# A new opening, a relieved VectorE at the convolution's end, and a later place for two sign conversions in a four-block transformer kernel

## The chip, the cores and the metric

The kernel runs on one core of a Trainium2 chip. The metric is device time in microseconds, lower is better. Before the change it takes 740.42 us (median of three runs, 739.88 to 740.97).

A core has five engines with a queue of instructions each, taken in order: TensorE (PE, matmuls and transposes), VectorE (DVE), ScalarE (ACT), GpSimd (POOL), and SyncE (SP), which here only issues DMAs. PEld is TensorE's loading of weights. Engines wait for each other by semaphores. Matmul results go to PSUM; everything else lies in SBUF or in device memory.

## The reference

The input `x` is 8 x 256 x 512, that is 2048 rows of 512. Four blocks follow each other, each added to x through the tanh of a gate:

```python
x = x + jnp.tanh(g_xattn[0]) * conv(ctx, ctx, layernorm(x), ssm_kernel, D)   # 32 heads of 8 channels
x = x + jnp.tanh(g_ffn[0]) * ffn0(layernorm(x), w1, w2, w3)                  # ternary weights, int8 rows
x = x + jnp.tanh(g_xattn[1]) * attention(layernorm(x), ctx, mask)            # 256 keys per batch
x = x + jnp.tanh(g_ffn[1]) * ffn1(layernorm(x), w1, w2, w3)                  # sign weights, int8 groups of 64
```

`conv` forms the products k_i * v_j of the 8 channels of a head, convolves each causally with the head's kernel of length 512, adds D times the product, multiplies by q (here the normalised x) and sums over i. `ffn0` is `(silu(a(x) W1) * (a(x) W2)) W3`; `a` rounds a row to int8 by its largest magnitude, and weights are rounded to -1, 0, 1 by their mean magnitude.

## The kernel before, in words

x lies in SBUF as 16 row tiles `xs[:, t, :]` of 128 rows. The even tiles hold the first half of each batch's sequence and feed heads 0 to 15, the odd ones feed heads 16 to 31.

**Opening (L606 to L713).** Eight even tiles are needed before the first head can be multiplied by q: each is loaded (`load_x`, in pairs), gets mean and variance on VectorE (`pair_stats`, L116 and L117), a root on ScalarE (`pair_sqrt`), a reciprocal and a bias on VectorE (`pair_inverse`), is normalised (`pair_norm` on ScalarE, or `ln_apply` on VectorE, L174), transposed by TensorE (`pair_turn`, L387) and copied from PSUM into `qT` (`pair_keep`). `load_ch` loads a head's context, `ctx_twice` (ScalarE, L290) and `pair_products` (GpSimd, L303 and L309) make its 36 products `kv`. `toep` is a Toeplitz view of a head's kernel, 128 x 512. Head 0 reads it from the input and gets D on its diagonal by `first_diagonal`; the others read `ssm_skip`, a copy in device memory to which D has been added. The written order of these calls is the order on every engine, since scheduling is manual (L217).

**Convolution (L716 to L748).** One pass per head h, with these calls in order: loads for h+3 and h+4; `q_twice(h+1)` and `ctx_twice(h+3)` on ScalarE, `pair_products(h+3)` on GpSimd; `half_products(h, 1)` on VectorE (three multiplies of y in PSUM by q, L348, L354, L361); the reduction of head h-1 on VectorE (L376), after `add_halves` on GpSimd (L371) had added the two halves of `prod`; heads 12, 14, 19 and 21 (`alone`) have no `add_halves` and one longer reduction on VectorE in their own pass (L378); `half_matmuls(h+1, 1)`, `half_wrap(h+1, 1)` (ScalarE, L336), `half_products(h+1, 0)`, `half_matmuls(h+2, 0)`, `half_wrap(h+2, 0)`. There are three PSUM buffers for y, so a half's matmuls wait for the VectorE products of the half three before. Between these calls stand jobs by head and slot (`job`, `run`): loading, summing and rounding of the ffn0 weights (`abs_w0`, `round_w0` on ScalarE, `clip_w0` on GpSimd), sums of ffn1 weights, odd tiles, adding finished tiles back to x, and towards the end the first rows of ffn0 (`front_norm`, `front_max`, `front_int`, `front_turn`) and statistics of eight tiles (`first_stats`, `ln_moments_of`).

**ffn0 (L923 to L1014).** One step per row tile t, 17 steps. Each has three `up_block` calls (TensorE L792, silu on ScalarE L800, gate on VectorE L801), the rounding of the row before (`row_max` on VectorE, int8 on ScalarE L942, `qh` in bf16 on GpSimd L960, a transposing DMA `hqT` L962), `down0` of the row two before (L809), and the front of the row two after. `ln_finish` makes inverse roots for four tiles by three Newton steps of small GpSimd instructions (L159 to L165). From step 3 on two 512-wide pieces of ffn1 weights are loaded per step (`w1_signs`) and turned into signs on ScalarE a step later (L780). Step 16 (t == NT) only rounds the last row and opens attention.

**Attention and ffn1 (L1118 to L1360)** are touched only by the order in which signs arrive.

Of the kernel before, what the change touches and what calls it, by code (L numbers as in the profile page):

```python
# [42 lines left out]
def flamingo_gated_kernel(  # L43
# [47 lines left out]
    nc.gpsimd.memset(ln_eps, LN_EPS)  # L91
    gates_in = small.tile([P, 4], F32, name="gates_in")
    gates = const.tile([P, 4], F32, name="gates")
# [148 lines left out]
    ssm = big.tile([H, P + L], F32, name="ssm")  # L242
    skip = big.tile([H, 1], F32, name="skip")
    d0 = big.tile([P, 1], F32, name="d0")

# [39 lines left out]
    def first_diagonal():  # L285
        t = toeps[0][:, :P]
        nc.vector.scalar_tensor_tensor(t, anti, d0[:, 0:1], t, op0=ALU.mult, op1=ALU.add)

# [84 lines left out]
    def reduce_terms(h, added):  # L373
# [3 lines left out]
        else:  # L377
            nc.vector.tensor_reduce(  # L378
                o, prod.rearrange("p k a j d -> p (a j) k d"), AX.XY, ALU.add
            )  # L380
# [70 lines left out]
    def clip_w0(i, k):  # L451
# [48 lines left out]
    def front_int(k):  # L500
        i80[k] = pf1.tile([P, L], I8, tag="i8x", name="i8x")
        nc.scalar.activation(i80[k], xn0.pop(k), AF.Copy, scale=am0[k][1])
# [68 lines left out]
    for i, (a, b, c) in enumerate(STEPS0):
        for k in range(NL):
            job(a + k, "load", load_w0, i, k)
            job(b + k, "act", abs_w0, i, k)
            job(c[k], "act", round_w0, i, k)
            job(c[k] if i < 2 else (29, 30, 31, 31)[k], "pool", clip_w0, i, k)
# [17 lines left out]
    for k in range(2):  # L594
# [3 lines left out]
        job(28 + k, "pool", front_turn, k)  # L598
    for k in range(GRP, 2 * GRP):
        job(24 + k, "dve", ln_moments_of, st0, order0, k, "0")  # L600

# [3 lines left out]

    for g, o in ((g_xattn, 0), (g_ffn, 2)):  # L606
        nc.scalar.dma_start(out=gates_in[:, o : o + 2], in_=g.partition_broadcast(P))
    nc.scalar.dma_start(out=d0, in_=ssm_d[0:1].partition_broadcast(P))
    nc.scalar.dma_start(out=ssm, in_=ssm_pad)
    nc.scalar.dma_start(out=skip, in_=ssm_d.rearrange("(h o) -> h o", o=1))  # L610
    pairs = [evens[k : k + 2] for k in range(0, len(evens), 2)]
    load_x(pairs[0])
    load_ch(0)
    first_toep()
    for k in range(1, len(pairs)):
        load_x(pairs[k])
    load_ch(1)
    load_table(AF.Tanh)
    nc.scalar.activation(gates, gates_in, AF.Tanh)
    load_table(AF.Sqrt)  # L620

    ps_ = {}
# [8 lines left out]

    def pair_inverse(k, by_act):

        mv, std = ps_[k]
        rstd = ln_inverse(std, 2, "p")
        nmr = ln_nmr(nc.vector, mv, rstd, by_act, "p")
        both = wl.tile([P, 3 * L], F32, tag="w0st", name="xnp")
        xn = [both[:, :L], both[:, L : 2 * L]]
        for j in range(2):
            if j not in by_act:  # L640
                ln_apply(xn[j], pairs[k][j], mv, rstd, j)
        ps_[k] = (xn, rstd, nmr)

    def pair_norm(k, by_act):
        xn, rstd, nmr = ps_[k]
        for j in by_act:
            ln_apply_act(xn[j], pairs[k][j], rstd, nmr, j)

    def pair_turn(k, js=(0, 1)):
        for j in js:  # L650
            transpose_x(pairs[k][j], ps_[k][0][j])

# [7 lines left out]
    pair_stats(0, 0)  # L660
    pair_stats(0, 1)
    ctx_twice(0)
    pair_products(0)
    pair_sqrt(0)
    pair_stats(1, 0)
    pair_inverse(0, (0, 1))
    pair_norm(0, (0, 1))
    first_diagonal()
    pair_stats(1, 1)
    pair_turn(0)  # L670
    pair_sqrt(1)
    half_matmuls(0, 0)
    nc.vector.tensor_add(ssm[:, P : P + 1], ssm[:, P : P + 1], skip)
    nc.sync.dma_start(out=ssm_skip, in_=ssm)
    load_toep(1)
    load_ch(2)
    load_toep(2)
    load_ch(3)
    pair_stats(2, 0)
    pair_keep(0, 0, nc.scalar)  # L680
    pair_inverse(1, (0,))
    pair_norm(1, (0,))
    pair_keep(0, 1, nc.scalar)
    pair_stats(2, 1)
    pair_turn(1, (1, 0))
    pair_sqrt(2)
    pair_stats(3, 0)
    half_matmuls(0, 1, (0,))
    pair_keep(1, 1, nc.scalar)
    pair_inverse(2, (0,))  # L690
    pair_norm(2, (0,))
    pair_stats(3, 1)
    pair_turn(2, (1, 0))
    pair_sqrt(3)
    pair_keep(1, 0, nc.scalar)
    pair_inverse(3, (0,))
    pair_norm(3, (0,))
    ctx_twice(1)
    pair_products(1)
    pair_keep(2, 1, nc.vector)  # L700
    half_wrap(0, 0)
    pair_turn(3, (1, 0))
# [13 lines left out]
    for h in range(H):  # L716
# [206 lines left out]
    for t in range(NT + 1):  # L923
# [484 lines left out]
```

## Time and profile before

| what | value |
|---|---|
| median of three runs | 740.42 us |
| the profiled execution | 740.89 us |
| its span, first to last instruction | 739.1 us |
| convolution, TensorE busy from 40 to 100 us | 58.85 of 60 us |
| the same from 160 to 220 us | 54.41 of 60 us |
| the same from 300 to 330 us | 26.41 of 30 us |
| the same from 420 to 440 us | 20.00 of 20 us |
| DMA rate from 5 to 10 us | 346 GB/s |

The span is 1.8 us shorter than the execution; what lies around it belongs to the start and end of the program. A row of the timeline gives the start, the duration, the engine and source line, the operation, the tile written and the tiles read with their shapes, and how many were merged. In brackets stands how long the engine had been idle before it and what ended that. "q" behind an engine's name means its sequencer, which issues DMAs. A busy TensorE is not always a fast one: equal matmuls can be compared by their duration.

### The profile page before, as it was taken

Reading aid. Unit: us, or ns where it says so; the run is one execution under the profiler, and the core shown is the slowest. Engines: PE = TensorE matmul, PEld = TensorE weight load, DVE = VectorE, ACT = ScalarE, POOL = GpSimd, SP = SyncE. Lnnn points to the kernel's source line nnn. Section 1 sums busy time; section 2 is a strip of 40 time slices with the busy share of each in tenths; the row PEclk is TensorE's granted clock in tenths of the full one; section 3 lists DMA queues with packets and bytes.
Section 4 is the critical chain, followed back from the end, with each engine's and each line's share of the span. In section 5 each row is a group of like instructions: output and inputs, shape, how many; then the busy total and the mean of one; then the engine's idle time right before and its main releaser. Section 6 shows DMA issues by size and latency. Waiting matters only on the chain.

```text
span 739.1 us, 10041 instructions
## 1 busy us (share of the span) xinstructions
PE 711.0 (96%) x3172; PEld 528.3 (71%) x3172; DVE 605.0 (82%) x1232; ACT 363.7 (49%) x640; POOL 255.8 (35%) x360
## 2 busy tenths in 40 slices
PE   4999999999899999989999999999999999999997
PEld 3777777776454444556677788888888888888885
DVE  4799878898988889667777999888889888777965
ACT  5477877765577777758851223222223322222322
POOL 2898988888885444343310010000200002000000
PEclk9999999999999999999999999999999999999999
DMA  5675676831055557778613455445444545553443
GB/s 193 208 234 173 186 255 197 270 96 43 15 84 137 138 138 157 167 232 254 200 57 55 101 122 125 96 108 118 108 95 97 121 90 118 109 115 82 109 88 85
DMA packets 150444, 99.36 MB, mean 134 GB/s; under 512 B 84280, under 2 KB 128312, under 8 KB 150392
## 3 DMA queue, kind: packets, MB, share of 16 engines
q1 hardware_dynamic: 149608, 98.38, 51.3%
q0 software_dynamic: 256, 0.26, 0.5%
q8 instruction: 25, 0.41, 0.2%
q14 instruction: 27, 0.22, 0.1%
q10 hardware_dynamic: 528, 0.08, 0.1%
HBM read 75.58 MB, written 5.03 MB: 109 GB/s over the span
## 4 chain that ended last, share of the span: by engine, by line
PE 66%; DVE 4%; DMA 3%; issue 1%; POOL 1%; ACT 1%; SPq 0%; DVEq 0%; ACTq 0%; POOLq 0%
PE po L1283 16%; PE pb L1098 15%; PE pa L1098 15%; PE po L809 4%; PE po L907 4%; PE pb L792 4%; PE pa L792 4%; PE ps L878 3%; DMA hqT<-qh 1%; DMA w1st<-in_L_w2t 1%; DMA sT<-d 1%; PE tr L867 1%; DVE hh L801 1%; DVE st L116 0%; DVE qT L376 0%
## 5 line engine op out<-in xcount | busy, mean ns | idle before, releaser
L326 PE MATMUL y<-kv,toep 128*128 128x288 f32 x640 | 162.5, 411 | 4.4 <-DVE prod L361 4.2
L326 PEld LDWEIGHTS y<-kv,toep 128*128 128x128 f32 x640 | 120.3, 192 | 37.7 <-issue 2.0
L1106 ACT ACTIVATE sl<-pa,wmean 128x512 f32<-128x512 f32 x64 | 44.0, 688 | 187.2 <-PE pa L1098 187.2
L1098 PE MATMUL pa<-w,hi 128*128 128x512 f32 x256 | 100.7, 393 | 0.0
L1098 PE MATMUL pb<-w,hi 128*128 128x512 f32 x256 | 99.9, 390 | 0.6 <-DVE hh L1110 0.6
L1283 PE MATMUL po<-w,lo 128*128 128x512 f32 x256 | 100.0, 391 | 0.0
L1283 PE MATMUL po<-w,hi 128*128 128x512 f32 x256 | 99.8, 390 | 0.0
L1098 PE MATMUL pa<-w,lo 128*128 128x512 f32 x256 | 99.7, 390 | 0.0
L1098 PE MATMUL pb<-w,lo 128*128 128x512 f32 x256 | 99.7, 389 | 0.0
L159 POOL TENSOR_TENSOR nwt<-rstd 128x4 f32<-128x4 f32 x33 | 6.5, 198 | 240.5 <-DVE rstd L154 238.8
L303 POOL TENSOR_TENSOR kv<-cx 128x1024 f32<-128x1024 f32 x32 | 60.6, 1893 | 33.9 <-ACT cx L290 33.9
L371 POOL TENSOR_TENSOR prod<-prod 128x1024 f32<-128x1024 f32 x28 | 66.2, 2363 | 2.7 <-DVE prod L361 2.7
L792 PEld LDWEIGHTS <-xqT 128*128 128x128 bf16 x384 | 37.4, 98 | 41.4 <-issue 4.5
L1073 ACT CAST hi<-v 128x512 fp32r<-128x512 f32 x64 | 39.1, 621 | 48.6 <-DVE v L1273 48.6
L1110 DVE SCALAR_TENSOR_TENSOR hh<-pb,wmean,sl 128x512 f32<-128x512 f32 x64 | 47.7, 746 | 14.1 <-PE pb L1098 14.1
L1098 PEld LDWEIGHTS pb<-w,hi 128*128 128x128 f32 x256 | 48.1, 188 | 11.0 <-DVE hh L1110 1.0
L1283 PEld LDWEIGHTS po<-w,lo 128*128 128x128 f32 x256 | 48.1, 188 | 10.8 <-DVE lo L1078 1.0
L1098 PEld LDWEIGHTS pa<-w,hi 128*128 128x128 f32 x256 | 48.1, 188 | 10.3 <-issue 0.5
L1098 PEld LDWEIGHTS pa<-w,lo 128*128 128x128 f32 x256 | 48.1, 188 | 10.3 <-DVE lo L1078 0.2
L1283 PEld LDWEIGHTS po<-w,hi 128*128 128x128 f32 x256 | 48.1, 188 | 9.9
L1098 PEld LDWEIGHTS pb<-w,lo 128*128 128x128 f32 x256 | 48.1, 188 | 9.9
L348 DVE TENSOR_TENSOR prod<-y,qx 128x512 f32<-128x512 f32 x64 | 43.6, 681 | 10.9 <-ACT y L336 7.1
(142 smaller groups left out, 1325.3 us busy)
## 6 DMA issues: line engine op xcount, KB each, us to landing
sT<-d SPq DMA_DIRECT2D x64, 256.0 KB
toep<-ssm_skip SPq DMA_DIRECT2D x31, 256.0 KB
ch<-in_ctx_heads SPq DMA_DIRECT2D x32, 128.0 KB
w1a<-in_L_w1t SPq DMA_DIRECT2D x8, 512.0 KB
w1a<-in_L_w2t SPq DMA_DIRECT2D x8, 512.0 KB
w1st<-in_L_w1t SPq DMA_DIRECT2D x16, 256.0 KB
w1st<-in_L_w2t SPq DMA_DIRECT2D x16, 256.0 KB
cT<-in_ctx_t SPq DMA_DIRECT2D x8, 512.0 KB
```

Of the source, the lines that this page charges most:

```text
L303: nc.gpsimd.tensor_tensor(kv[:, :, 0 : ND * HD].rearrange("p a (i d) -> p a i d", d=ND), cx[:, :, 0:HD].unsqueeze(3).to_broadcast([P, NL * ...
L326: nc.tensor.matmul(y[:, k, :, W0 : W0 + NPAIR], toeps[h][:, d * P : (d + 1) * P], kvs[h][:, mi * B : (mi + 1) * B, :].rearrange("p b n -> ...
L348: nc.vector.tensor_tensor(prod[:, 0, r, :, :], yv[:, :, W0 : W0 + ND * HD].rearrange("p a (i d) -> p a i d", d=ND), view(q, [HX, n], [1, H ...
L371: nc.gpsimd.tensor_tensor(flat[0], flat[0], flat[1], ALU.add)
L792: nc.tensor.matmul(pp[:, :fw], xqT[:, c, :], w0q[i][:, c, f0 : f0 + fw], start=(c == 0), stop=(c == NL - 1),)
L809: nc.tensor.matmul(po, hqT[:, c, :], w0q[2][:, c, :], start=(c == 0), stop=(c == NF0 - 1))
L907: nc.tensor.matmul(po, eT[:, c, :], cN[:, c, :], start=(c == 0), stop=(c == S // P - 1))
L1073: nc.scalar.copy(hi, v)
L1098: nc.tensor.matmul(pp, xT[k][:, c, :], w1q[i][:, c, f0 : f0 + 512], start=(c == 0 and k == 0), stop=(c == NL - 1 and k == 1),)
L1106: nc.scalar.activation(sl, pa, AF.Silu, scale=wmean1[:, 0:1])
L1110: nc.vector.scalar_tensor_tensor(hh, pb, wmean1[:, 1:2], sl, op0=ALU.mult, op1=ALU.mult)
L1283: nc.tensor.matmul(po, hT[b][k][:, c, :], w1q[2][:, b * NL + c, :], start=(b == 0 and c == 0 and k == 0), stop=(b == NB - 1 and c == NL - ...
```

## The change

It has six parts.

- Opening, loads: the two gate broadcasts, the broadcast of D[0] and the column `skip` are replaced by three loads into one row, `singles`; two small matmuls spread it over partitions (`wide`). The x pairs are issued ahead of `toep` of head 0.
- Opening, work: 18 matmuls of `ident` by itself on TensorE (`warm`), with nothing that reads their result. `pair_norm` puts a tile on ScalarE, GpSimd or VectorE; tiles (1,1) and (2,1) go to GpSimd. The tanh of the gates moves into the first head's pass.
- Reductions of the heads in `alone` move one pass later; the last head's reduction moves from VectorE in ffn0's first step to GpSimd in the last pass (`reduce_last`).
- Statistics of four tiles move from VectorE (passes 28 to 31) to ScalarE (passes 24, 25, 28, 29; `moments_by_act`, five instructions a tile).
- The second `i8x` gets a tile of its own; the last `clip_w0` becomes a Sign on ScalarE.
- ffn0: `down0` of row 0 moves behind the third `up_block` of step 2; the pending signs of step 16 are made in attention's first step; `batch_gate` moves from step 15 to step 16.

```diff
+    def moments_by_act(got, order, k, tag, junk):
+        g, j = k // GRP, k % GRP
+        if g not in got:
+            got[g] = small.tile([P, GRP, 2], F32, tag="mv" + tag, name="mv")
+        mean, var = got[g][:, j, 0:1], got[g][:, j, 1:2]
+        v = xs[:, order[k], :]
+        st = small.tile([P, nc.vector.BN_STATS_DIM], F32, tag="st", name="st")
+        nc.scalar.activation(junk, v, AF.Identity, accum_out=st[:, 0:1])
+        nc.scalar.activation(st[:, 1:2], st[:, 0:1], AF.Copy, scale=-1.0 / L)
+        nc.scalar.activation(junk, v, AF.Square, bias=st[:, 1:2], accum_out=st[:, 2:3])
+        nc.scalar.activation(mean, st[:, 0:1], AF.Copy, scale=1.0 / L)
+        nc.scalar.activation(var, st[:, 2:3], AF.Copy, scale=1.0 / L)
...
+    def reduce_last(h):
+        prod, o = prods.pop(h), qT[:, :, h * HD : (h + 1) * HD]
+        half = prod[:, 1, :, :, 0:2]
+        nc.gpsimd.tensor_tensor(half, prod[:, 0, :, :, 0:2], prod[:, 0, :, :, 2:4], ALU.add)
+        nc.gpsimd.tensor_tensor(o, half[..., 0], half[..., 1], ALU.add)
...
+    def clip_by_act(i, k):
+        n, a = FW[i][k], sum(FW[i][:k])
+        q = w0q[i].rearrange("p c f -> p (c f)")
+        nc.scalar.activation(q[:, a : a + n], w0r.pop((i, k))[:, :n], AF.Sign)
...
-        i80[k] = pf1.tile([P, L], I8, tag="i8x", name="i8x")
+        i80[k] = (big if k == 1 else pf1).tile([P, L], I8, tag="i8x", name="i8x")
...
+    job(0, "act", tanh_gates)
+    job(1, "act", load_table, AF.Sqrt)
...
-    for k in range(GRP, 2 * GRP):
-        job(24 + k, "dve", ln_moments_of, st0, order0, k, "0")
+    for k, h in enumerate((24, 25, 28, 29)):
+        job(h, "late", first_by_act, GRP + k)
...
-    for g, o in ((g_xattn, 0), (g_ffn, 2)):
-        nc.scalar.dma_start(out=gates_in[:, o : o + 2], in_=g.partition_broadcast(P))
-    nc.scalar.dma_start(out=d0, in_=ssm_d[0:1].partition_broadcast(P))
     nc.scalar.dma_start(out=ssm, in_=ssm_pad)
-    nc.scalar.dma_start(out=skip, in_=ssm_d.rearrange("(h o) -> h o", o=1))
+    for v, o in ((ssm_d, 4), (g_xattn, 0), (g_ffn, 2)):
+        n = v.shape[0]
+        nc.scalar.dma_start(out=singles[:, o : o + n], in_=v.rearrange("(o n) -> o n", o=1))
     pairs = [evens[k : k + 2] for k in range(0, len(evens), 2)]
     load_x(pairs[0])
     load_ch(0)
-    first_toep()
     for k in range(1, len(pairs)):
         load_x(pairs[k])
+    first_toep()
     load_ch(1)
-    load_table(AF.Tanh)
-    nc.scalar.activation(gates, gates_in, AF.Tanh)
     load_table(AF.Sqrt)
+    pt = ps_tr.tile([P, 512], F32, tag="tr", name="warm")
+    def warm(n):
+        for _ in range(n):
+            nc.tensor.matmul(pt[:, :P], ident, ident, start=True, stop=True)
+    warm(8)
+    wide = ps_tr.tile([P, 512], F32, tag="tr", name="wide")
+    nc.tensor.matmul(wide[:, : 4 + H], ones[0:1, :], singles, start=True, stop=True)
+    nc.tensor.matmul(
+        wide[:H, 64:65], singles[:, 4 : 4 + H], ones[0:1, 0:1], start=True, stop=True
+    )
+    warm(10)
...
     pair_stats(0, 0)
     pair_stats(0, 1)
+    nc.vector.tensor_copy(wide_sb, wide[:, : 4 + H])
+    nc.vector.tensor_add(ssm[:, P : P + 1], ssm[:, P : P + 1], wide[:H, 64:65])
+    nc.sync.dma_start(out=ssm_skip, in_=ssm)
     ctx_twice(0)
     pair_products(0)
...
-        if h > 0 and h - 1 not in alone:
-            reduce_terms(h - 1, True)
-        if h in alone:
-            reduce_terms(h, False)
-        else:
+        if h > 0:
+            reduce_terms(h - 1, h - 1 not in alone)
+        if h not in alone:
             add_halves(h)
...
+        if h == H - 1:
+            reduce_last(h)
         run(h, "pool")
...
             load_table(AF.Exp)
-            for make in signs:
-                make()
-            signs = []
+            gates3 = {0: batch_gate(negs[0])}
...
-        if t >= 2:
+        if t > 2:
             hqT, f3 = hq_.pop(t - 2)
             d_[t - 2] = (down0(hqT), f3)
...
+        if t == 2:
+            hqT, f3 = hq_.pop(0)
+            d_[0] = (down0(hqT), f3)
...
         if t == 0:
-            reduce_terms(H - 1, True)
+            clip_by_act(2, 3)
...
-        for make in signs:
-            make()
-        signs = []
+        if t < NT:
+            for make in signs:
+                make()
+            signs = []
...
-            gates3 = {0: batch_gate(negs[0])}
```

The rest of the opening after `pair_products(0)` is written anew, in this order of TensorE's work: turns of tiles (0,0), (0,1), (1,1), (1,0), the first half of head 0, turn (2,1), a third of its second half, turns (2,0), (3,1), (3,0), and the rest of head 0. Before, it was turns (0,0), (0,1), the first half, turns (1,1), (1,0), part of the second, then the turns of pairs 2 and 3 and the rest.

More of the change, by code (lines that the diff above doesn't have):

```diff
@@ L91, in flamingo_gated_kernel @@
     nc.gpsimd.memset(ln_eps, LN_EPS)
-    gates_in = small.tile([P, 4], F32, name="gates_in")
+    const.tile([P, 24], F32, name="lines")
     gates = const.tile([P, 4], F32, name="gates")
@@ L242, in flamingo_gated_kernel @@
     ssm = big.tile([H, P + L], F32, name="ssm")
-    skip = big.tile([H, 1], F32, name="skip")
-    d0 = big.tile([P, 1], F32, name="d0")
+    singles = big.tile([1, 4 + H], F32, name="singles")
+    wide_sb = big.tile([P, 4 + H], F32, name="wide_sb")
+    d0 = wide_sb[:, 4:5]
     anti = wl.tile([P, 3 * L], F32, tag="w0st", name="anti")[:, :P]
@@ L286, in first_diagonal @@
         t = toeps[0][:, :P]
-        nc.vector.scalar_tensor_tensor(t, anti, d0[:, 0:1], t, op0=ALU.mult, op1=ALU.add)
+        nc.vector.scalar_tensor_tensor(t, anti, d0, t, op0=ALU.mult, op1=ALU.add)
     def twice(out, src):
@@ L566, in flamingo_gated_kernel, with tanh_gates @@
         job(k + 5, "act", keep_x, odds[k])
+    def tanh_gates():
+        load_table(AF.Tanh)
+        nc.scalar.activation(gates, wide_sb[:, 0:4], AF.Tanh)
+    job(0, "act", tanh_gates)
+    job(1, "act", load_table, AF.Sqrt)
     for k in range(len(evens)):
@@ L575, in flamingo_gated_kernel @@
             job(c[k], "act", round_w0, i, k)
-            job(c[k] if i < 2 else (29, 30, 31, 31)[k], "pool", clip_w0, i, k)
+            if (i, k) != (2, 3):
+                job(c[k] if i < 2 else (29, 30, 31)[k], "pool", clip_w0, i, k)
         job(b + NL - 1, "dve", total_w0, i)
@@ L598, in flamingo_gated_kernel, with first_by_act @@
         job(28 + k, "pool", front_turn, k)
-    for k in range(GRP, 2 * GRP):
-        job(24 + k, "dve", ln_moments_of, st0, order0, k, "0")
-    for g, o in ((g_xattn, 0), (g_ffn, 2)):
-        nc.scalar.dma_start(out=gates_in[:, o : o + 2], in_=g.partition_broadcast(P))
-    nc.scalar.dma_start(out=d0, in_=ssm_d[0:1].partition_broadcast(P))
+    def first_by_act(k):
+        junk = p2.tile([P, L], F32, tag="xn", name="junk")
+        moments_by_act(st0, order0, k, "0", junk)
+    for k, h in enumerate((24, 25, 28, 29)):
+        job(h, "late", first_by_act, GRP + k)
     nc.scalar.dma_start(out=ssm, in_=ssm_pad)
-    nc.scalar.dma_start(out=skip, in_=ssm_d.rearrange("(h o) -> h o", o=1))
+    for v, o in ((ssm_d, 4), (g_xattn, 0), (g_ffn, 2)):
+        n = v.shape[0]
+        nc.scalar.dma_start(out=singles[:, o : o + n], in_=v.rearrange("(o n) -> o n", o=1))
     pairs = [evens[k : k + 2] for k in range(0, len(evens), 2)]
@@ L630, in pair_sqrt, with pair_inverse, pair_norm, pair_turn @@
         ps_[k] += (ln_sqrt(ps_[k][0], 2, "p"),)
-    def pair_inverse(k, by_act):
+    def pair_inverse(k):
         mv, std = ps_[k]
         rstd = ln_inverse(std, 2, "p")
-        nmr = ln_nmr(nc.vector, mv, rstd, by_act, "p")
+        nmr = ln_nmr(nc.vector, mv, rstd, range(2), "p")
         both = wl.tile([P, 3 * L], F32, tag="w0st", name="xnp")
[L638 to L644, printed above, removed]
+        ps_[k] = ([both[:, :L], both[:, L : 2 * L]], rstd, nmr)
+    def pair_norm(k, j, eng):
         xn, rstd, nmr = ps_[k]
-        for j in by_act:
+        if eng is nc.scalar:
             ln_apply_act(xn[j], pairs[k][j], rstd, nmr, j)
-    def pair_turn(k, js=(0, 1)):
-        for j in js:
-            transpose_x(pairs[k][j], ps_[k][0][j])
+        else:
+            c = slice(j, j + 1)
+            eng.tensor_scalar(
+                xn[j], xs[:, pairs[k][j], :], rstd[:, c], nmr[:, c], ALU.mult, ALU.add
+            )
+    def pair_turn(k, j):
+        transpose_x(pairs[k][j], ps_[k][0][j])
     def pair_keep(k, j, eng):
@@ L664, in flamingo_gated_kernel @@
     pair_sqrt(0)
+    pair_inverse(0)
+    pair_norm(0, 0, nc.scalar)
+    pair_norm(0, 1, nc.scalar)
     pair_stats(1, 0)
-    pair_inverse(0, (0, 1))
-    pair_norm(0, (0, 1))
+    pair_stats(1, 1)
+    pair_turn(0, 0)
+    pair_turn(0, 1)
+    pair_sqrt(1)
+    pair_stats(2, 0)
+    pair_inverse(1)
+    pair_keep(0, 0, nc.scalar)
+    pair_keep(0, 1, nc.scalar)
+    pair_norm(1, 1, nc.gpsimd)
+    pair_norm(1, 0, nc.scalar)
+    pair_stats(2, 1)
     first_diagonal()
-    pair_stats(1, 1)
-    pair_turn(0)
-    pair_sqrt(1)
+    pair_turn(1, 1)
+    pair_turn(1, 0)
     half_matmuls(0, 0)
-    nc.vector.tensor_add(ssm[:, P : P + 1], ssm[:, P : P + 1], skip)
-    nc.sync.dma_start(out=ssm_skip, in_=ssm)
     load_toep(1)
@@ L678, in flamingo_gated_kernel @@
     load_ch(3)
[L679 to L685, printed above, removed]
     pair_sqrt(2)
     pair_stats(3, 0)
-    half_matmuls(0, 1, (0,))
[L689 to L693, printed above, removed]
-    pair_sqrt(3)
[L695 to L702, printed above, removed]
+    pair_inverse(2)
+    pair_keep(1, 1, nc.scalar)
+    pair_keep(1, 0, nc.scalar)
+    pair_norm(2, 1, nc.gpsimd)
+    ctx_twice(1)
+    pair_norm(2, 0, nc.scalar)
+    pair_products(1)
+    pair_stats(3, 1)
+    pair_turn(2, 1)
+    half_matmuls(0, 1, (0,))
+    pair_turn(2, 0)
+    pair_sqrt(3)
+    pair_inverse(3)
+    pair_norm(3, 1, nc.vector)
+    pair_norm(3, 0, nc.scalar)
+    pair_keep(2, 1, nc.scalar)
+    pair_turn(3, 1)
+    pair_turn(3, 0)
     pair_keep(2, 0, nc.vector)
-    pair_keep(3, 1, nc.scalar)
-    pair_keep(3, 0, nc.vector)
+    pair_keep(3, 1, nc.vector)
+    pair_keep(3, 0, nc.scalar)
     half_matmuls(0, 1, (1,))
     q_twice(0)
+    half_wrap(0, 0)
     half_wrap(0, 1)
```

## The prediction

> **What bounds the kernel now.** I read the page's busy table first, then the waits of TensorE, then the timeline around each place where TensorE stands still.
>
> ```profile
> span 739.1 us, 10041 instructions
> ...
> PE 711.0 (96%) x3172; PEld 528.3 (71%) x3172; DVE 605.0 (82%) x1232; ACT 363.7 (49%) x640; POOL 255.8 (35%) x360
> ```
>
> TensorE is the bound: a change gains only what it takes out of TensorE's standstill, or out of time in which TensorE runs slowly. The timeline shows four places. First the opening:
>
> ```profile
> 0.73 0.46 SPq L260 DMA_DIRECT2D xs<-in_x  x1
> ...
> 4.30 2.26 SPq L260 DMA_DIRECT2D xs<-in_x  x3
> ...
> 5.68 0.69 DVE L116 BATCH_NORM_STATS2 st<-xs 128x6 f32<-128x512 f32 x1 [5.68 <-DMA xs<-in_x]
> ...
> 8.73 0.69 DVE L116 BATCH_NORM_STATS2 st<-xs 128x6 f32<-128x512 f32 x1 [1.35 <-DMA xs<-in_x]
> ...
> 10.93 1.94 PE L387 MATMUL tr<-ident,xnp 128*128 128x128 f32 x8 [10.93 <-ACT xnp L179]
> ...
> 12.66 3.09 PE L326 MATMUL y<-kv,toep 128*128 128x288 f32 x6
> ...
> 17.09 1.62 PE L326 MATMUL y<-kv,toep 128*128 128x288 f32 x6
> ...
> 22.71 0.69 DVE L348 TENSOR_TENSOR prod<-y,qx 128x512 f32<-128x512 f32 x1 [0.74 <-ACT qx L290]
> ```
>
> TensorE does nothing for 10.9 us; then six equal matmuls take 3.09 us and later 1.62 us: it runs at half speed until about 16.9 us, though the clock column reads 1.00. From 21.08 us it is full. The second and third row pairs are issued 3 us after the loads before them: SyncE stood until an earlier load had landed.
>
> Second, the heads in `alone`, where VectorE does two reductions in a row before the product that frees a y buffer (TensorE's waits, us, times, longest; then the timeline):
>
> ```profile
> PE y L326 <- DVE prod L361: 4.2, 6, 1.5
> ```
> ```profile
> 136.24 1.22 DVE L376 TENSOR_REDUCE qT<-prod 128x256 f32<-128x1024 f32 x1 [1.74 <-POOL prod L371]
> ...
> 137.38 2.28 DVE L378 TENSOR_REDUCE qT<-prod 128x256 f32<-128x2048 f32 x1
> ...
> 141.09 5.09 PE L326 MATMUL y<-kv,toep 128*128 128x288 f32 x20 [1.48 <-DVE prod L361]
> ```
>
> Third, the convolution's end, where VectorE is busy from 136 to 201 us but for one hole:
>
> ```profile
> 179.05 0.72 ACT L502 ACTIVATE i8x<-xn,sc 128x512 int8<-128x512 f32 x1 [3.95 <-POOL qx L506]
> ...
> 180.02 0.69 DVE L348 TENSOR_TENSOR prod<-y,qx 128x512 f32<-128x512 f32 x1 [1.60 <-ACT y L336]
> ```
> ```profile
> 200.77 0.81 PE L792 MATMUL pb<-w,xqT 128*128 128x384 bf16 x4 [1.30 <-DVE hh L801]
> ...
> 207.62 2.55 PE L809 MATMUL po<-w,hqT 128*128 128x512 bf16 x11 [0.99 <-DMA hqT<-qh]
> ```
>
> Fourth, the step into attention, where two sign conversions stand ahead of the last row of integers:
>
> ```profile
> 311.42 1.27 ACT L780 ACTIVATE w<-w1st 128x512 fp32r<-128x512 f32 x2 [1.45 <-DMA w1st<-in_L_w2t]
> ...
> 314.60 0.44 PE L899 MATMUL tre<-ident,s 128*128 128x128 f32 x2 [1.08 <-ACT s L893]
> ```
> ```profile
> 319.06 2.55 PE L809 MATMUL po<-w,hqT 128*128 128x512 bf16 x11 [1.14 <-DMA hqT<-qh]
> ```
>
> From 325 us on TensorE is full, so what is gained before comes out at the end.
>
> **Part 1, the opening: -3.4 us (-1 to -5).** The three broadcasts to 128 partitions and the skip column go; three single-row loads take their place. With two SyncE loads ahead of it instead of three, pair 1 goes out at about 1.75 us and pair 2 at 2.2, without a wait in the listing; pair 3 waits for the ssm rows. The loads ran at 346 GB/s between 5 and 10 us, so a pair (0.52 MB) takes 1.5 us. I take the first pair at 5.0 us (4.7 without the tiny packets ahead of it, 5.7 if nothing changes), then 6.9, 8.4 and 9.9, toep 10.6. VectorE's chain from 5.0: two statistics of 0.82 and a copy and an add of about 0.3 (nearest: 0.13 and 0.21 for tiny operations), 6.95; square root 0.29, reciprocal 0.13 and two of 0.17 with hand-overs, 7.5. ScalarE normalises two tiles at 0.75 each to 9.0, takes a root (0.3) and two copies (0.58), 10.5, and tile (1,0), 11.3. Statistics of pairs 1 to 3 lie under this. TensorE then turns (1,0) by 12.3, and runs six matmuls (1.46), a turn (0.44), six more and a turn: 16.1. The copy of (2,0) waits for VectorE and takes 0.7; the last turn 0.44 and its delay: the last four matmuls of head 0 start at 17.7, where before they started at 21.08. First product 19.3 for 22.71. The chain of ch, toep and kv for heads 1 to 3 moves forward with it: ssm_skip is written at about 7 us instead of 11.21.
>
> GpSimd's two normalisations have no row. The nearest in size is 128x512 int8 (0.61 us), the nearest in arithmetic 128x256 from uint8 to f32 (1.08, so 2.16 for 512). I take 0.8; 2.16 would cost 1.1, since `pair_turn` of that tile stands ahead of its neighbour. Table loads: one more (1.28 us and 0.2), but the tanh and the second root load move into heads 0 and 1, where ScalarE idled 2.04 us ahead of its copy of y: nothing on the path, 1.7 if that idle time is gone.
>
> The 18 warm matmuls (two records of 0.21 us each cold, from the turns' 1.94 for eight) fill 1.5 to about 9 us. [...] The row: work from 10.93, full speed at 16.9, so 6 us. By the row the clock opens at about 7.5[...]. Warm, the 17.7 holds; if it opens only at 10, the queue of warm matmuls itself delays the first turn to 9.7 and costs 1.2; if never, twelve matmuls and the turns cost 3.
>
> New waits: the `wide` matmuls wait for the small loads, and VectorE's copy waits for them, with all later statistics queued behind it. The nearest row is the tanh at 5.92 us, released by such a load behind 256 tiny packets; VectorE gets there at 6.65, so 0.7 us of cover; each microsecond beyond it costs one. `first_diagonal` waits for toep (10.6) and stands ahead of pair 3's statistics; VectorE gets there at 11.
>
> **Part 2, reductions of lone heads one head later: -1.1 (0 to -2.8).** Same instruction (2.28 us), other place. TensorE's standstill is 1.1 us at head 12, 0.2 at head 14, 1.45 at head 21. Behind heads 12 and 14 VectorE has idle time (1.6 us each), so 1.3 comes free. Behind head 21 VectorE is full to 178 us; what TensorE gains there it waits for by 172. I take 1.1.
>
> **Part 3, the end of the convolution: -3.3 (0 to -4.5).** VectorE loses four pairs of statistics (4 x 0.82 = 3.3) and the last reduction (1.21). A buffer of its own for the second i8x takes away ScalarE's 3.95 and so VectorE's 1.60. ScalarE gains four calls of five instructions: 0.63 + 0.19 + 0.2 + 0.72 + 0.19 and two of 0.2, overlapped by 0.1 (from the 1024-wide row of 1.06 + 0.19, and the 0.2 of one element): 2.1 us, four times. They stand ahead of the q copy and ctx copy of the next head. In heads 24 and 25 ScalarE idled 1.03 and 1.07 us ahead of its y copies, so a call pushes the ctx copy, hence kv, add_halves and the reduction, by about 0.4 in the end. In 28 and 29 the q copy ends at 180.7 and 186.1 instead of 180.7 and 184.3; the product of head 31 is ready at 187.5 instead of 188.7.
>
> GpSimd's reduction of the last head: 512 adds and 256 adds. Rows: 1024 in 1.89 to 2.36, 512 in 1.27, so 1.9. [...] Behind it on GpSimd stand a clip (1.47), the turn of row 2 (0.9), the Newton steps (3.9) and the first qh (1.36): that ends at 200.9 instead of 203.0, so hqT lands at 205.5 (4.6 later, as before). The moved down-projection now stands behind 1.3 us of other matmuls; it starts at 205.5 and row 2 ends at 208.4 instead of 211.75. The last clip as a sign on ScalarE (1.1) lies in its 2.3 us of idle time at 192.
>
> **Part 4, into attention: -2.2 (-0.5 to -3).** The last i8h no longer waits behind the signs and `batch_gate` (0.62): 309.6 instead of 312.59. qh, hqT, ctx and w1st loads queued behind it on SyncE move with it by 2.5 to 3. The exponentials then wait for VectorE's mask (311.7), so the first tre goes from 314.6 to 313.5; the two signs still stand ahead of the first eT copy (314.3 for 315.15). The wait of 1.14 for hqT goes. Of 3.5 us standstill between 310 and 324.4, 2.2 go.
>
> Sum: 3.4 + 1.1 + 3.3 + 2.2 = 10.0. Against the profiled execution's own 740.9 us this is 730.9; the median of the runs lies 0.5 lower: 730.4.
>
> **Rivals.** (A, 0.50) as summed, 730.4, own range 727.5 to 732.5. (B, 0.20) the opening gives 1 instead of 3.4, clock late or GpSimd slow: 732.8; [...]against it, 7 us of matmuls. (C, 0.14) ScalarE's calls hold the q copies of heads 24 to 31, and part 3 gives 0.5: 733.2; for it, 2.1 is as much as ScalarE's idle time in a head. (D, 0.10) head 21's 1.45 us and the rest of part 3 come free too: 727.5. (E, 0.06) slower: the four calls are fully exposed. From the point at which ScalarE has no idle time left in a head, each costs its whole 2.1, together 8.4, and part 3's gain is gone: 740.9 - 6.7 + 8.4 - 0.5 = 742.1. Against it, heads 28 and 29 have no ctx copy.
>
> The measurement tells 0.2% (1.5 us) from no change. Faster: A to D, 0.93; E split into 0.04 slower and 0.02 within. One more hundredth goes to the middle from C. Range 726.5 to 734.5, which takes in B, C and D.
>
> **What would show it.** Opening: first VectorE statistics near 5, second pair released near 7 and not 8.7, first six y matmuls in about 1.6 us, first L348-type product near 19.3. Lone heads: no TensorE gap near heads 12 and 21. End: no ScalarE wait of 4 us for i8x; the first projection matmul 1.2 us sooner than the opening's shift alone; hqT released by GpSimd's Newton steps. Attention: no sign between the last sc and the last i8h. Wrong if TensorE shows new gaps behind ScalarE's q copy in heads 25 to 31, or the first turns run at half speed.

## The result and the profile after

The changed kernel takes 730.5 us (median of four runs, 728.5 to 733.8) where the kernel before takes 740.15 in the runs beside it: a ratio of 0.987 [0.984, 0.991] (after over before; in brackets the 95% interval). The forecast was 730.4. Two lines from the top of the page of the changed kernel's profile:

```profile
span 728.0 us, 10153 instructions
...
PE 716.1 (98%) x3212; PEld 533.8 (73%) x3212; DVE 602.4 (83%) x1224; ACT 373.8 (51%) x672; POOL 258.4 (36%) x363
```

TensorE has 40 matmul records more than before, two for each of 20 matmuls (711.0 us busy, now 716.1), and a span that is 11.1 us shorter: busy time grew and the time fell, since what went is standstill and half speed. To see where, I read in every timeline when TensorE reaches the same piece of work:

| start, us | before | after | moved by | share of the stage | forecast |
|---|---|---|---|---|---|
| last four matmuls of head 0 | 21.08 | 18.34 | -2.74 | -2.7 | -3.4 |
| y of head 23 | 142.62 | 136.58 | -6.04 | | |
| y of head 29 | 173.96 | 169.45 | -4.51 | -1.8 | -1.1 |
| row 3 of ffn0 | 211.75 | 203.03 | -8.72 | -4.2 | -3.3 |
| end of the last matmul | 735.24 | 724.04 | -11.20 | -2.5 | -2.2 |

The "share" is the step from the last line that has one. The four parts give 11.2 in the profiled executions, where 10.0 was forecast. The medians lie 9.6 apart: the profiled execution before lies 0.7 us above its median, that after 0.8 below.

**Opening**, from the timeline of the changed kernel:

```profile
1.46 3.78 PE L664 MATMUL warm<-ident 128*128 128x128 f32 x16 [1.46 <-POOL ln_eps L91]
...
4.73 0.69 DVE L118 BATCH_NORM_STATS2 st<-xs 128x6 f32<-128x512 f32 x1 [4.73 <-DMA xs<-in_x]
...
5.99 4.31 PE L664 MATMUL warm<-ident 128*128 128x128 f32 x20
...
7.25 0.69 DVE L118 BATCH_NORM_STATS2 st<-xs 128x6 f32<-128x512 f32 x1
...
10.14 1.04 PE L410 MATMUL tr<-ident,xnp 128*128 128x128 f32 x8
...
10.45 0.77 POOL L697 TENSOR_SCALAR xnp<-xs,rstd,nmr 128x512 f32<-128x512 f32 x1 [2.39 <-DVE nmr L136]
...
13.11 1.62 PE L343 MATMUL y<-kv,toep 128*128 128x288 f32 x6
...
18.34 2.83 PE L343 MATMUL y<-kv,toep 128*128 128x288 f32 x11
...
20.02 0.69 DVE L365 TENSOR_TENSOR prod<-y,qx 128x512 f32<-128x512 f32 x1 [1.46 <-ACT y L353]
```

The second pair's statistics (7.25) no longer wait for a DMA, and the first six y matmuls take 1.62 us instead of 3.09. But the 36 warming records took 0.21 us each nearly to their end: full speed came at 9.8. The first tile was normalised by 8.0; its turn stood behind the queue of warming matmuls until 10.14.

**Heads.** TensorE's waits between 20 and 185 us:

```profile
PE pa L852 <- DVE prod L378: 1.0, 1, 1.0
PE y L343 <- DVE rstd L128: 0.8, 1, 0.8
PE y L343 <- ACT y L353: 0.4, 1, 0.4
PE y L343 <- DVE prod L378: 0.2, 1, 0.2
```

The waits of 1.1 and 1.5 us at heads 12 and 21 are gone. The first line was there before (1.1 us), and so was the fourth. The second, at 167 us, was 0.2 and is 0.8, and the third, at 161, is new. By head 29 the convolution has given back 1.5 of the 6.0 us that it had won by head 23, most of it at these two places.

**From the convolution to row 3**, TensorE's timeline:

```profile
193.14 0.81 PE L852 MATMUL pb<-w,xqT 128*128 128x384 bf16 x4 [0.63 <-DVE hh L861]
...
200.22 2.54 PE L869 MATMUL po<-w,hqT 128*128 128x512 bf16 x11
...
203.03 1.03 PE L852 MATMUL pa<-w,xqT 128*128 128x512 bf16 x4
```

The first `down0` waits for nothing. Of 1.30 us at `pb` 0.63 is left.

**Into attention**, TensorE again:

```profile
304.71 0.38 PE L959 MATMUL tre<-ident,s 128*128 128x128 f32 x2
...
308.20 2.55 PE L869 MATMUL po<-w,hqT 128*128 128x512 bf16 x11
```

Both waited before (1.08 and 1.14 us).

### The profile page after: what moved, and what is told of

Read it like the earlier page. It is cut to its first block, busy times and chain, and to the rows that moved or that the text cites. A ratio compares the mean times of both kernels' runs of the same rounds, so it can differ in the third digit from the quotient of the medians.

```text
span 728.0 us, 10153 instructions
## 1 busy us (share of the span) xinstructions
PE 716.1 (98%) x3212; PEld 533.8 (73%) x3212; DVE 602.4 (83%) x1224; ACT 373.8 (51%) x672; POOL 258.4 (36%) x363
## 4 chain that ended last, share of the span: by engine, by line
PE 88%; DVE 4%; DMA 2%; ACT 2%; issue 1%; POOL 1%; SPq 0%; DVEq 0%; ACTq 0%
PE y L343 20%; PE po L1345 16%; PE pb L1160 15%; PE pa L1160 15%; PE po L869 5%; PE po L967 4%; PE pa L852 4%; PE pb L852 4%; PE ps L938 3%; PE tr_back L418 1%; DMA hqT<-qh 1%; DMA w1st<-in_L_w3t 1%; DVE am L512 1%; PE tr L927 1%; PE tr L410 1%
## 5 line engine op out<-in xcount | busy, mean ns | idle before, releaser
L343 PE MATMUL y<-kv,toep 128*128 128x288 f32 x640 | 160.7, 407 | 1.6 <-DVE rstd L128 0.8
L1160 PEld LDWEIGHTS pa<-w,hi 128*128 128x128 f32 x256 | 48.1, 188 | 10.4 <-issue 0.5
```

Of the source, the lines that this page charges most:

```text
L343: nc.tensor.matmul(y[:, k, :, W0 : W0 + NPAIR], toeps[h][:, d * P : (d + 1) * P], kvs[h][:, mi * B : (mi + 1) * B, :].rearrange("p b n -> ...
L1160: nc.tensor.matmul(pp, xT[k][:, c, :], w1q[i][:, c, f0 : f0 + 512], start=(c == 0 and k == 0), stop=(c == NL - 1 and k == 1),)
```

## The experiments

Marks and gaps are from each kernel's own profiled execution, and "the mark" alone is the start of the last four matmuls of head 0; medians move by a microsecond or two from run to run, so sizes below two microseconds are read from the marks. By how much a mark itself varies can be seen from two profiles of the changed kernel (the second is the run `after_again`): from the mark at head 0 to head 29 they differ by 0.2 us, from there to row 3 by 0.2, from row 3 to attention by 0.4.

### Is it the clock or the loads? Three kernels

```diff
-    warm(8)
...
-    warm(10)
```

> The changed kernel without its 18 warming matmuls; the two `wide` matmuls stay. Theory W (the warmed TensorE gives the opening's gain): the first turn can start at about 8.1 us instead of 10.14, but TensorE then reaches full speed only some 6 us later, as in the kernel before; the first six y matmuls take about 3.1 us instead of 1.62, the last four matmuls of head 0 start at 19.5 to 20 instead of 18.34, and the time is 731.7 to 732.5. Rival L (the order of the loads and the shorter VectorE chain give it, and the warming costs as much as it brings, since the first turn waits behind it): the last four matmuls start at 18.3 or earlier, and the time is 729.5 to 730.5.

Measured: 732.6 us (731.3 to 733.4). TensorE's timeline:

```profile
8.55 1.94 PE L410 MATMUL tr<-ident,xnp 128*128 128x128 f32 x8 [2.43 <-ACT xnp L195]
...
13.73 3.08 PE L343 MATMUL y<-kv,toep 128*128 128x288 f32 x6
...
20.52 3.80 PE L343 MATMUL y<-kv,toep 128*128 128x288 f32 x15
```

The turns start 1.6 us earlier than with the warming, but they and the six y matmuls run at half speed; the last four start at 20.52, half a microsecond later than W gave. All the rest of the new opening is worth 0.56 us without the warming. L falls. The reverse, the old opening with warming alone:

```diff
     load_table(AF.Sqrt)
+    pt = ps_tr.tile([P, 512], F32, tag="tr", name="warm")
+    for _ in range(28):
+        nc.tensor.matmul(pt[:, :P], ident, ident, start=True, stop=True)
```

> The kernel before with only 28 warming matmuls ahead of its first turn. Theory W (of the opening's gain most is the clock): its first turns start at 10.95 as before, but at full clock; the first six y matmuls take 1.62 us instead of 3.09, the first product starts at 20.5 to 21.3 instead of 22.71; 738.4 to 739.2. Rival L (without the earlier loads TensorE only waits longer for the later pairs): the last four matmuls of head 0 stay at 20.8 or later; 739.7 to 740.2. If the warming ends so early that the clock falls back, six y matmuls of 3.1 us would show it.

Measured: 738.4 us, a ratio of 0.998 [0.997, 0.999]. TensorE's timeline:

```profile
1.46 9.25 PE L623 MATMUL warm<-ident 128*128 128x128 f32 x56 [1.46 <-POOL ln_eps L91]
...
12.03 1.62 PE L326 MATMUL y<-kv,toep 128*128 128x288 f32 x6
...
19.03 3.32 PE L326 MATMUL y<-kv,toep 128*128 128x288 f32 x13
```

The warming alone moves the mark by 2.05 us, from 21.08 to 19.03, and the other edits alone by 0.56: together 2.6 of the 2.74. W is right. The third kernel shortens the queue of warming matmuls so that the first turn need not stand behind it. In the changed kernel the second row of warming began at 5.99 us, and full speed came at 9.82, inside it: that row is what theory G counts on, and here it is half as long.

```diff
-    warm(10)
+    warm(5)
```

> The changed kernel with 5 instead of 10 warming matmuls behind `wide`, so that the queue of them ends near 8.1 us, when the first normalised tile is there (8.0), and not at 10.14. Theory Q (the clock opens after enough work in all): it opens later by about the time that TensorE then stands still, the first turns start at 8.1 and the last four matmuls of head 0 at about 17.5; 729.7. Theory G [...]: now the stretch ends near 9.2 behind the turns of pair 0 and the opening comes late; the first six y matmuls take about 3 us, and the last four start at 19 or later; 731 to 732.

Measured: 730.7 us (729.3 to 732.8). TensorE's timeline:

```profile
5.80 1.38 PE L664 MATMUL warm<-ident 128*128 128x128 f32 x10
8.13 1.36 PE L410 MATMUL tr<-ident,xnp 128*128 128x128 f32 x8 [0.95 <-ACT xnp L195]
11.38 1.97 PE L410 MATMUL tr<-ident,xnp 128*128 128x128 f32 x8 [1.89 <-POOL xnp L697]
13.14 2.40 PE L343 MATMUL y<-kv,toep 128*128 128x288 f32 x6
...
15.81 1.62 PE L343 MATMUL y<-kv,toep 128*128 128x288 f32 x6
...
19.14 5.26 PE L343 MATMUL y<-kv,toep 128*128 128x288 f32 x21
```

The mark is late, as G said, but neither Q nor G had foreseen how. The ten records behind `wide` take 1.38 us, so this execution was at full speed from 4.5 us; the turns at 11.38 are slow again, behind 1.9 us of standstill; in the middle of the six matmuls, at 14.7, it is fast once more. The profile's own record of the clock agrees: half speed from 11.3 to 14.7. Ahead of that standstill lie the turns of 8.13 (1.36 us). Up to `wide` the two kernels have the same warming matmuls from 1.46 us on, and yet one reached full speed at 4.5 and the other at 9.8. So the moment may differ from one execution of the same opening to the next, and the break at `wide` may play a part; the next two runs try both.

### One unbroken row of warming, and the changed kernel again

```diff
-    warm(8)
+    warm(18)
     wide = ps_tr.tile(...)
...
-    warm(10)
...
     pair_stats(1, 0)
+    nc.vector.tensor_copy(wide_sb, wide[:, : 4 + H])
```

(The last line and the two behind it are moved down from ahead of `ctx_twice(0)`.)

> The changed kernel with all 18 warming matmuls ahead of `wide` in one unbroken row, and the copy of `wide` behind one more statistics on VectorE. Theory G [...]: full clock always between 4.4 and 8.3 us and not at 9.8 to 10.6; the first turn at 8.1, the last four matmuls of head 0 at 16.8 to 17.5 instead of 18.34; 729. Rival C (the clock needs about 8 us from the first matmul, or so many matmuls): opens at 9.4 or later, the last four at 18.3.

TensorE's timeline:

```profile
11.90 1.09 PE L410 MATMUL tr<-ident,xnp 128*128 128x128 f32 x8 [2.20 <-POOL xnp L696]
...
18.06 6.23 PE L343 MATMUL y<-kv,toep 128*128 128x288 f32 x25
```

Full speed came at 6.6 us, inside G's range, which was the author's estimate, and ahead of C's 9.4: C falls. But the mark is 18.06, and the time 731.3 us (730.9 to 731.9): VectorE now waits 0.6 us for `wide`, GpSimd's tile comes at 11.08 instead of 10.45 and the second pair's turns at 11.90. What the clock gave, the order of VectorE took.

The changed kernel once more, with no edit:

> The changed kernel once more, beside the others on one chip, for its spread and for another sample of when full clock comes. [...]full clock somewhere between 4.4 and 10.7 us, the last four matmuls of head 0 between 17.3 and 18.9, the time between 728.5 and 734. With a fixed delay from the first matmul: 9.8 again.

Measured: 730.9 us (729.2 to 731.3), full speed from 10.4, mark at 18.59. Seven of the kernels run have the opening of the changed kernel to the letter. By the record of the clock, which agrees with the durations of the matmuls, they reach full speed at 5.8, 9.5, 9.5, 9.8, 10.0, 10.4 and 10.7 us, with the mark at 17.32, 18.16, 18.32, 18.34, 18.38, 18.59 and 18.87. A fixed delay falls. The early one is the kernel `signs_ahead`, whose other edit lies at 300 us:

```profile
6.07 2.50 PE L664 MATMUL warm<-ident 128*128 128x128 f32 x20
...
17.32 1.38 PE L343 MATMUL y<-kv,toep 128*128 128x288 f32 x5
```

The other six reached it at 9.5 to 10.7, 3.5 us or more after 6.0, where the break at `wide` ends (5.99 in the changed kernel; up to 0.28 us idle and 0.7 us of small matmuls). The three kernels whose row is unbroken, `warm_before`, `warm_straight` and `best`, reached full speed at 7.2, 6.6 and 7.4. But a break alone does not make it late: `signs_ahead` had one too (0.24 us idle ahead of 5.49) and was at full speed at 5.8, with the small matmuls still to end. What sets the moment is not shown by these runs.

### The reductions of lone heads by themselves

```diff
-        if h > 0 and h - 1 not in alone:
-            reduce_terms(h - 1, True)
-        if h in alone:
-            reduce_terms(h, False)
-        else:
+        if h > 0:
+            reduce_terms(h - 1, h - 1 not in alone)
+        if h not in alone:
             add_halves(h)
```

> The kernel before with only the reductions of the four lone heads moved behind the next head's second half. Theory P (as predicted): 1.3 us free at heads 12 and 14, and the 1.45 us of head 21 is won and then lost by head 27 to a full VectorE; y matmuls at 142.6 come 2.5 to 3.3 us earlier, those at 174 only 1.1 to 1.8; 738.5 to 739. Rival K (all is kept, VectorE has room): 737 at most. Rival N (nothing is kept, since the end of the convolution is bound by VectorE in the kernel before): 739.9 to 740.2.

Measured: 738.6 us, a ratio of 0.998 [0.997, 0.999]. The y of head 23 start at 139.23, 3.4 us earlier than before; those of head 29 at 172.47, 1.5 earlier; ffn0 starts 1.75 earlier. P holds; K and N fall. TensorE's waits from 20 to 185 us:

```profile
PE y L326 <- DVE prod L361: 1.1, 2, 0.8
PE y L326 <- DVE rstd L126: 0.8, 1, 0.8
```

Here ScalarE has no statistics, and yet the standstill of 0.8 us at 170 us is there. It belongs to the reductions' move.

### The end of the convolution, three parts undone

First the four statistics go back to VectorE:

```diff
-    for k, h in enumerate((24, 25, 28, 29)):
-        job(h, "late", first_by_act, GRP + k)
+    for k in range(GRP, 2 * GRP):
+        job(24 + k, "dve", ln_moments_of, st0, order0, k, "0")
```

> The changed kernel with the four row statistics back on VectorE, in heads 28 to 31. Theory V (they are worth what they free on VectorE): 0.82 us each, of which part lies in VectorE's hole of 1.1 us at head 31; the first projection starts 2 to 2.5 us later than 182.67 and the time is 732 to 733. Rival S (ScalarE's calls in heads 24 and 25 cost the 1.5 us that TensorE gives back between 157 and 173 us): TensorE's gaps of 0.36 and 0.79 us at 161.3 and 167.1 are gone, the y matmuls at 169.45 come 1 to 1.5 us earlier, and the time is 730 to 731. If VectorE alone makes those gaps, they stay as they are.

Measured: 733.4 us (730.6 to 734.4); the profiled run, 733.3, has a mark at head 0 that is 0.5 later, by its clock (full speed at 10.7 instead of 9.8). TensorE's gaps at 162, 168 and 174 us are 0.16, 0.80 and 0.20, so ScalarE's calls cost 0.2 us at the first of them and nothing at the others: S falls. The first projection comes 0.3 us later, counted from the opening's mark, not 2 to 2.5. From head 29 to row 3 it takes 34.87 us instead of 33.58, so the statistics are worth 1.3 us, all of it behind the first projection, where TensorE waits for VectorE's gate (`hh`):

```profile
188.31 0.81 PE L852 MATMUL pb<-w,xqT 128*128 128x384 bf16 x4 [0.55 <-DVE hh L861]
...
192.56 1.02 PE L852 MATMUL pb<-w,xqT 128*128 128x512 bf16 x4 [0.71 <-DVE hh L861]
```

In the changed kernel the first of these waits is missing, and the second is 0.23. V has the direction, not the size or the place.

Next, the last reduction back behind row 0's projections:

```diff
-        if h == H - 1:
-            reduce_last(h)
...
         if t == 0:
+            reduce_terms(H - 1, True)
             clip_by_act(2, 3)
```

> The changed kernel with the reduction of head 31 back on VectorE, behind row 0's projections (1.21 us there). Theory G (GpSimd's reduction is what lets the integers of row 2 start early): row 3 starts 1 to 1.5 us later than in the changed kernel, counted from the first projection; span 729 to 729.5 at an equal opening. Rival N (the reduction lies beside other work on either engine, and the earlier start of row 3 comes from the four statistics and the moved down-projection): within 0.4 us.

Measured: 730.2 us (729.9 to 730.9); head 29 to row 3 33.66 us, 0.08 more than with the change, which is less than two profiles of one kernel differ. N holds. Why so little is in three timelines, VectorE's and GpSimd's of the changed kernel and VectorE's of this one:

```profile
187.54 0.65 DVE L166 TENSOR_SCALAR nwv<-mv 128x4 f32<-128x4 f32 x1
188.22 1.40 DVE L168 TENSOR_SCALAR nwi<-nwv 128x4 int32<-128x4 int32 x1
189.65 0.17 DVE L170 TENSOR_SCALAR rstd<-nwi 128x4 int32<-128x4 int32 x1
```
```profile
187.51 0.65 POOL L403 TENSOR_TENSOR qT<-prod 128x256 f32<-128x256 f32 x1
188.13 1.47 POOL L477 TENSOR_SCALAR w<-w0r 128x1536 bf16<-128x1536 int8 x1
```
```profile
187.60 0.24 DVE L166 TENSOR_SCALAR nwv<-mv 128x4 f32<-128x4 f32 x1
187.88 0.17 DVE L168 TENSOR_SCALAR nwi<-nwv 128x4 int32<-128x4 int32 x1
188.09 0.47 DVE L170 TENSOR_SCALAR rstd<-nwi 128x4 int32<-128x4 int32 x1
```

Two VectorE instructions on four elements last until GpSimd's instruction beside them ends (189.62 and 189.60 for the second). From the start of the first to the end of the third are 2.28 us, and 0.96 with the reduction on VectorE. So VectorE is spared 1.21 us and loses 1.3. Why the two end together is not shown.

Third, one buffer for both i8x again, and `down0` of step 2 back ahead of the third `up_block`:

```diff
-        i80[k] = (big if k == 1 else pf1).tile([P, L], I8, tag="i8x", name="i8x")
+        i80[k] = pf1.tile([P, L], I8, tag="i8x", name="i8x")
...
-        if t > 2:
+        if t >= 2:
             hqT, f3 = hq_.pop(t - 2)
...
-        if t == 2:
-            hqT, f3 = hq_.pop(0)
-            d_[0] = (down0(hqT), f3)
```

> The changed kernel with the second i8x in the shared buffer again and row 2's down-projection back ahead of the last up-projections. As predicted: ScalarE waits up to 4 us for the buffer, VectorE's product of head 30 and TensorE with it about 0.8 us near 175 us, and a wait of about 1.2 us for hqT comes back near 199; row 3 starts 1.5 to 2.2 us later, counted from the matmuls at 169.45. Rival N: with the four statistics off VectorE the buffer's wait falls into a hole and costs nothing, and only the down-projection's wait of 1.2 shows.

Measured: 734.2 us (732.2 to 736.4). ScalarE's timeline, then TensorE's:

```profile
174.59 0.72 ACT L531 ACTIVATE i8x<-xn,sc 128x512 int8<-128x512 f32 x1 [4.27 <-POOL qx L535]
```
```profile
179.77 3.63 PE L343 MATMUL y<-kv,toep 128*128 128x288 f32 x14 [0.89 <-ACT w0r L470]
...
201.60 1.69 PE L869 MATMUL po<-w,hqT 128*128 128x512 bf16 x7 [2.25 <-DMA hqT<-qh]
```

Head 29 to row 3 takes 35.96 us, 2.4 more. Both waits are back, the second larger than foreseen (2.25 for 1.2). The two edits were undone together; 1.2 us of the 2.4 come ahead of the first projection, where the buffer is used, and 1.2 behind it. The 1.3, 0.1 and 2.4 us add up to 3.8 of the 4.2.

### Signs ahead of the last integers

The signs and `batch_gate` go back to where the kernel before has them:

```diff
         if t == NT:
...
-            gates3 = {0: batch_gate(negs[0])}
+            for make in signs:
+                make()
+            signs = []
...
         if t == NT - 1:
             negs = {0: key_mask(bytes_.pop(0))}
+            gates3 = {0: batch_gate(negs[0])}
```

> The changed kernel with the two sign conversions and the gate of batch 0 back ahead of the last row of integers. Theory S (as predicted, the order gives 2.2): the last i8h comes some 2 us later counted from row 3's start, TensorE's standstill between 294 and 330 us goes from 1.15 us to about 3.5. Rival F (the earlier standstill was that of hqT, which the other parts have removed already): the standstill grows by less than 0.7 us.

Measured: 731.7 us (730.9 to 732.8), with the luckiest opening of all. TensorE's timeline:

```profile
304.57 0.44 PE L959 MATMUL tre<-ident,s 128*128 128x128 f32 x2 [0.57 <-ACT s L953]
...
309.04 2.55 PE L869 MATMUL po<-w,hqT 128*128 128x512 bf16 x10 [1.14 <-DMA hqT<-qh]
...
315.19 1.98 PE L967 MATMUL po<-cN,eT 128*128 128x512 f32 x4 [1.22 <-ACT eT L961]
```

The wait of 1.14 us for hqT is back to the hundredth. Standstill from 290 to 335 us is 4.1 us, for 1.2 in the changed kernel. S holds. This stage varies: over the ten profiles with the new order it is 1.1 to 3.2 us (median 1.8), over the four with the old order 3.4 to 4.1.

### A better version, which failed

The statistics of rows 2 and 3 leave the full heads:

```diff
-    for g, h in enumerate((22, 25)):
+    for g, h in enumerate((22, 29)):
```

> The changed kernel with the statistics of rows 2 and 3 (two of 0.82 us on VectorE) moved from heads 25 and 26 to 29 and 30, and what follows them with them, into VectorE's holes at 177 and 180 us. Theory V (a full VectorE makes TensorE's gaps of 0.36, 0.79 and 0.20 us at 161, 167 and 173 us): the last two gaps go, the first projection starts 0.6 to 1 us earlier, counted from the first product. Rival E (the end of the convolution hangs on ScalarE's q copy of head 31, released behind a statistics call): the gaps go, but a new one of as much stands before the first projection.

Measured: 731.5 us (730.7 to 734.2). The y of head 29 come 0.75 us earlier and ffn0 1.17, as V says; then TensorE stands 1.23 us at 185, since the norm of row 2, first in ScalarE's step 0, waits for VectorE's bias. E is right. Then all of it together, with the warming in one row, `wide` in a y buffer of its own and VectorE's work of the opening in another order:

```diff
-    for g, h in enumerate((22, 25)):
+    for g, h in enumerate((22, 28)):
...
-    warm(8)
+    warm(18)
...
     pair_stats(1, 1)
+    pair_sqrt(1)
+    nc.vector.tensor_copy(wide_sb, wide[:, : 4 + H])
...
+    pair_inverse(1)
...
     pair_stats(2, 0)
```

> The changed kernel with three edits: the 18 warming matmuls in one row ahead of `wide`, which gets a y buffer of its own; VectorE takes a pair's reciprocal ahead of the next pair's statistics, and the copy of `wide` while it would wait for the root; the statistics of rows 2 and 3 move from heads 25 and 26 to 28 and 29. If VectorE's order, and not the clock alone, holds the opening once the warming is unbroken, the second pair's turns start near 10.7 us (11.90 in the kernel with the warming in one row only) and the last four matmuls of head 0 at 16.8 to 17.3; behind head 23 TensorE's gap of 0.79 us goes without the new one of 1.23 at 185 us, as the norm of row 2 no longer waits for VectorE; together 728.3 to 729. If the opening is held by the loads, the last four start at 18 or later and 730 comes out.

Measured: 732.8 us (732.2 to 733.7), slower than the changed kernel. The turns of the second pair did start at 10.74. But then, VectorE's, GpSimd's and TensorE's timeline:

```profile
15.89 2.09 DVE L696 TENSOR_SCALAR xnp<-xs,rstd,nmr 128x512 f32<-128x512 f32 x1
```
```profile
15.80 1.89 POOL L320 TENSOR_TENSOR kv<-cx 128x1024 f32<-128x1024 f32 x1 [1.71 <-ACT cx L307]
```
```profile
18.13 1.16 PE L410 MATMUL tr<-ident,xnp 128*128 128x128 f32 x8 [2.15 <-DVE xnp L696]
```

VectorE's normalisation, 0.68 us in the changed kernel, started 0.09 us behind the start of a GpSimd multiply and took 2.09. In all eleven profiles of the new opening it ends 0.28 or 0.29 us behind the end of that multiply; in the changed kernel it starts 0.4 us before the multiply's end. In the kernel before, where GpSimd stood idle from 10.64 to 20.06, a normalisation of the same size took 0.54 (L174, at 12.22). The mark came at 19.13.

Even so ffn0 starts 1.3 us earlier than in the changed kernel (181.37 for 182.67). At the start of ffn0 TensorE stood 2 us, behind VectorE's product of head 31, which now had the row's reciprocal ahead of it. And the standstill cost again: behind it TensorE ran at half speed for 3.4 us (184.9 to 188.3), so that half of them, 1.7 us, is lost by estimate. In the second row below, which is of a stretch and not of an instruction, the granted clock is the third number from the end.

```profile
184.38 1.38 PE L851 MATMUL pb<-w,xqT 128*128 128x512 bf16 x4 [1.99 <-DVE prod L378]
```
```profile
185.00:188.30 3.30, 3.30 (x9) 1.22 (x8) 2.11 (x5) 0.99 (x3) 3.14 (x3) 0.50 0.02 5
```

At row 3 the kernel is 1.0 us behind the changed one; most of the other two are standstill near attention (3.0 us for 1.2). No version here beats the changed kernel.

## Why the forecast held, step by step

- **The bound.** Right: every microsecond gained is standstill or half speed of TensorE.
- **Opening, -3.4; measured -2.74.** Loads (first statistics at 5.0, measured 4.73; no wait at pair 1), GpSimd's normalisation (0.8, measured 0.77) and the cover of `wide` held. The step that failed: "By the row the clock opens at about 7.5". The row of before, 6 us from first work to full speed, was one draw and not a fixed delay: one opening reached full speed 4.3 to 9.2 us after its first matmul. That the gain came out so near is luck in part: it compares one draw with one draw, and the seven marks of the new opening lie 2.2 to 3.8 us before that of the old. The forecast had its price: opening at 10 "costs 1.2". Full speed at 9.8 gives 3.4 - 1.2 = 2.2, and 2.74 came. Nor had the forecast seen how much of the 3.4 is clock: three quarters.
- **Lone heads, -1.1; measured -1.5 to -1.8.** "What TensorE gains there it waits for by 172" is what `lone_only` shows, 3.4 us at head 23 and 1.5 at head 29.
- **End of the convolution, -3.3; measured -4.2.** The statistics were given 1.2 by way of head 31's product, and brought 1.3. ScalarE's call takes 1.95 us (156.48 to 158.43), forecast 2.1. GpSimd's two adds take 1.7 us (1.04 and 0.65; the forecast's rows gave 1.9), and gain nothing. Per element of a row the second, which reads every 16 bytes, took 2.5 ns and the first 2.0. The term that was too small is what follows: the buffer and the moved `down0` bring 2.4.
- **Into attention, -2.2; measured -2.5.** The hqT wait went; by the median of ten profiles against four it is nearer 2.
- **Rivals.** B (clock late, opening gives 1) had the right cause and too high a price. C and E are out: with ScalarE's calls taken away TensorE's gaps change by 0.2 us at most. D is out in head 21 (`lone_only`); in its other half, more from the convolution's end, it was right by 0.9.

The errors of the parts (0.7 too much; 0.7, 0.9 and 0.3 too little) partly cancel, and the profiled execution lies 0.8 us below its median; the forecast is closer to the median than its terms were to theirs.

**Open.** The changed kernel's runs spread over 5 us. The moment of full speed, 5.8 to 10.7 us in one opening, moves the mark by 1.6, the standstill near attention varies by 2.1: its waits are those for hqT near 296 (0.3 to 1.3 us) and for eT near 316 (0 to 1.4), and what makes them vary wasn't tried. A third part shows in the mean granted clock: the slowest run, 733.8, has 0.995, the other three 0.999 to 1.000, and the slowest runs of `stats_vector`, `stats_late` and `i8x_down` have 0.995 too. As an estimate, 0.004 of 733 us is 3 us lost to half speed. Where these runs fell back isn't known, as they have no profile; `best` shows such a place, and its five runs have 0.994 to 0.998. The loads, GpSimd's normalisations and the last clip were not undone one by one.

## What to carry to other kernels

Warming matmuls ahead of the first real work paid 2 us here where the rest of the new opening alone paid 0.6. An unbroken row brought full speed by 7.4 us where a broken one mostly needed 9.5 or more, though no version with one was faster as a whole; with a shorter row (`warm_5`) TensorE fell back to half speed behind a wait of 1.9 us. Where TensorE stands for 2 us, look at the clock behind it: it can cost again (`best`). Before a piece of work is taken off a full engine, look whether the time won is waited for later on the same engine (head 21), and whether the first one then takes longer beside the engine that takes it (`reduce_last`: 1.21 us spared, 1.3 lost). A gain of a microsecond or two is read from where a stage starts in the profile, not from a median whose opening is a draw.

## What was not expected of the hardware

- The granted clock in the profile reads 1.00 in the opening, while equal matmuls take 0.48 and then 0.24 us: its record begins with the first change. Later losses it does show (0.50 in `best`).
- Full speed came 3.0 to 9.2 us after the first matmul, in kernels whose warming matmuls are the same up to 4.8 us. It was lost again behind a standstill of 1.9 us in `warm_5` and of 2.0 in `best`, and not behind one of 2.2 in `warm_straight`.
- A four-element VectorE instruction took 1.40 us instead of 0.17, and a 512-wide one 2.09 instead of 0.68, beside one GpSimd instruction; both ended just behind it.
